# Bias rows and masks made on the chip, and normalisation factors read in longer rows and earlier, in a two-layer kernel

## The chip, the cores and the metric

The kernel runs on one core of one Trainium2 chip. The metric is the device time of one execution in microseconds (us). A core has TensorE (PE, matrix products), VectorE (DVE), ScalarE (ACT), GpSimd (POOL) and SyncE (SP); SP, ACT and POOL also issue transfers (DMA) between DRAM and the on-chip memory SBUF. PSUM holds the results of matrix products. PE's share of full clock that the throttle granted is called the granted clock.

## What is computed

The input `x` is a picture of 512 x 512 positions with 64 channels. Two layers follow one another, each as `x = x + layer(groupnorm(x))`. Only the first layer's part matters here:

```python
xn = _ln(gn(x), norm_w, norm_b)          # over the 64 channels
mask = m[:, :, None] * m[:, None, :]     # m: 0 or 1 for each of 512 rows
left  = (xn @ left_w  + left_b)  * mask * sigmoid(xn @ lgate_w + lgate_b)
right = (xn @ right_w + right_b) * mask * sigmoid(xn @ rgate_w + rgate_b)
out_gate = sigmoid(xn @ ogate_w + ogate_b)
out = einsum('bkjd,bkid->bijd', left, right)
out = _ln(out, onorm_w, onorm_b) @ out_w + out_b
return out * out_gate
```

The second layer takes 12 x 12 low Fourier modes of its input, mixes their channels and transforms them back. Everything is in 32-bit floats.

## The kernel before

About half of the mask is zero, and `left` and `right` vanish wherever a row or column of the mask does. The kernel ranks the rows with a mask of one ahead of the others and gives them *slots*; if there are at most K = 256 of them it takes the path `compact` (line 628), which is the path of every run here. It works in stages that pass their results through DRAM. Within a stage the order of the instructions on each engine is the order of the code (`manual_schedule`): every engine and every queue works off its own list, and waits where a tile that it needs isn't there.

**Indices** (lines 58 to 137, the first 16 us): ranks of the rows by small matrix products, `slot_t` (for each slot the row's number, its mask and Fourier factors) and `src_i` (addresses for gathers).

**Stage 1** (lines 683 to 770): 16 iterations `jc`, each over 32 columns. POOL issues four indirect gathers of 1 MB an iteration (`gather`, L645), two iterations ahead: two into `xg` (the 256 slots), two into `yg` (the other rows). PE transposes all of them (L758) into six PSUM banks, DVE takes statistics of each bank (L759). The slots' columns that have a slot themselves stay in SBUF: `keep` (L740) copies 32 columns of `xg` into `xc`, at addresses read from registers, 22 of them by ACT (SHARE) and 10 by POOL. These dynamic copies write one tile, so ACT's and POOL's batches wait for one another in turn.

Beside that the weights are made. SP loads them (`load_weights`, L148, L167, L168: 28 small transfers). In iterations 5 to 8 ACT scales a weight matrix by the norm's factors (L702) and PE centres it (L707 to L709); in iteration 10 `keep_weights` (L711) copies them out of PSUM, and `b_all`, one column for each of four bias vectors. Two of these (`ogate`, `out`) are also needed as rows, the same in all partitions: SP writes the column to DRAM (`b_d`, L721, 64 writes of 4 bytes) and reads it back to all 128 partitions (`bias_row_...`, L723), twice; then it writes the row of `out` to slot K of `u_d` (L725). In the same way, at the stage's start, the mask of the slots goes from a column of `slot_t` to DRAM (`m_d`, L687, 256 elements of 4 bytes), and back as a row in all partitions (`mask_s`, L688) and as two columns (`mask_own`, L689). SP issues the weights' loads behind these.

**Stage 2** (lines 772 to 916): 64 groups `q` of four slots' columns (each a tile of 128 partitions x 512; a partition is a channel of one of two halves `r`). The loop runs from q = -14 to 63, with `lead` = 13:

- `channels(q+14)` (PE transposes L796, ACT applies the group norm L806),
- `centered(q+13)` (PE L817, ACT squares L821), and DVE sums the squares into `total` (L906),
- after each four groups `factors` puts nine small DVE steps of a reciprocal root on a list `todo`, of which each iteration does three,
- `spread(k)` (QB = 4 groups at once): PE turns the 32 x 128 factors (L834, into the PSUM tile `rc_ps`), ACT copies them (L836), POOL writes them to DRAM (`rs_d`, L838) and reads them back to 64 partitions for each half (`rbc`, L842: 64 x 4 rows of 2 KB for a half, 512 KB), into one of two tiles,
- `normed(q+1)`: DVE multiplies with `rbc` (L849),
- `project`: PE makes `gates` and `sides` (L855), ACT the sigmoid (L880), DVE adds the bias and multiplies (L901), and SP stores `left_d` and `right_d` (L913, 256 KB each) out of one of five tiles `o_c`.

Ahead of the loop the group norm's last steps run (`group_norm_affine`), beside which PE transposes the first six groups (`turn_x`). In the first loop iterations with q >= 0 a list `prepare` is worked off on DVE, one entry each.

**Stage 3** (lines 921 to 982): for each of 64 channels, load both sides (L932), transpose, multiply, mask by `mask_own` and `mask_s` (L967), store to `tri_d`. **Stage 4** normalises that, projects it, gates and adds it to `x` column by column, and takes the Fourier sums on the way; **stage 5** transforms back and writes the output.

Of the kernel before, what the change touches and what calls it, by code (L numbers as in the profile page):

```python
# [17 lines left out]
P = 128  # L18
N = 512
C = 64  # L20
# [11 lines left out]
K = 2 * P  # L32
AHEAD = 15
SHARE = 22
QB = 4
# [11 lines left out]
def conv_preact_kernel(ctx: ExitStack, tc: tile.TileContext, t: dict):  # L47
    nc = tc.nc
    x, out = t["x"], t["out"]

    const = ctx.enter_context(tc.tile_pool(name="const", bufs=1))
    dram = ctx.enter_context(tc.tile_pool(name="dram", bufs=1, space=DRAM))
# [575 lines left out]
    def compact(fc):  # L628
# [53 lines left out]
        with tc.tile_pool(name="wt", bufs=1) as cp:  # L682
            with tc.tile_pool(name="f1", bufs=1) as sp, tc.tile_pool(name="f1x", bufs=2) as xp, tc.tile_pool(
                name="f1y", bufs=4
            ) as yp, tc.tile_pool(name="f1p", bufs=6, space=PSUM) as pt, tc.manual_schedule():
                m_d = dram.tile([K], F32, name="m_d")
                nc.sync.dma_start(m_d.rearrange("(b p) -> p b", p=P), slot_t[:, : K // P, 1])  # L687
                nc.sync.dma_start(mask_s, m_d.unsqueeze(0).to_broadcast([P, K]))  # L688
                nc.sync.dma_start(mask_own, m_d.rearrange("(p b) -> p b", b=2))  # L689
                loaded, _ = load_weights(cp, nc.sync)  # L690
                mkp = ExitStack()
                mk = mkp.enter_context(tc.tile_pool(name="mk", bufs=1, space=PSUM))
# [18 lines left out]
                def keep_weights():  # L711

                    for i, (name, nw, nb, raw, b, k) in enumerate(loaded):
                        weights[name] = raw if i < 2 else fc.tile([P, P], F32, name="w_" + name)
                        nc.scalar.copy(weights[name], made[:, i, :])
                        biases[name] = b_all[:, i : i + 1]
                    nc.scalar.copy(b_all, made_b)
                    mkp.close()
                    b_d = dram.tile([2, C], F32, name="b_d")
                    for i, name in enumerate(("ogate", "out")):  # L720
                        nc.sync.dma_start(b_d[i].rearrange("(c o) -> c o", o=1), biases[name][:C])  # L721
                        rows_of[name] = fc.tile([P, C], F32, name="bias_row_" + name)
                        nc.sync.dma_start(rows_of[name], b_d[i].unsqueeze(0).to_broadcast([P, C]))  # L723
                    for r in range(2):
                        nc.sync.dma_start(u_d[:, K, r, :], rows_of["out"])  # L725

                sets = chunk_sets(fc, 4, 1)
                quarter = NJ // 4
# [15 lines left out]
                for jc in range(NJ):  # L744
                    if jc % quarter == 0:
                        stats = sp.tile([P, 1, 16 * quarter, 6], F32, name="stats1c")
                    if 0 <= jc - 5 < 4:
                        scale_weights(jc - 5)
                    if jc == 10:
                        keep_weights()  # L750
                    for r in range(4):
                        flat = xgs[jc][1][r].rearrange("p j c -> p (j c)")
                        for c in range(4):

                            ps = pt.tile([P, 4, P], F32, name="x_ps")
                            for i in range(4):
                                o = (8 * c + 2 * i) * C
                                nc.tensor.transpose(ps[:, i, :], flat[:, o : o + P], ident)  # L758
# [3 lines left out]
                    if 0 <= jc - 5 < 4:  # L762
                        center_weights(jc - 5)
                    keep(mybir.EngineType.Activation, nc.scalar.copy, jc, 0, SHARE)
                    keep(mybir.EngineType.Pool, nc.gpsimd.tensor_copy, jc, SHARE, JC)
                    del xgs[jc]
                    if jc + 2 < NJ:
                        fetch_tile(jc + 2)
                    if jc % quarter == quarter - 1:
                        join_chunks(sp, sets, jc // quarter, stats)  # L770

            rs_d = dram.tile([K // 4, 2, 4 * P], F32, name="rs_d")
            with tc.tile_pool(name="fn", bufs=2) as np_, tc.tile_pool(name="fw", bufs=2) as wk, tc.tile_pool(
                name="fr", bufs=3
            ) as rp, tc.tile_pool(name="fg", bufs=1) as sp, tc.tile_pool(name="fo", bufs=5) as op, tc.tile_pool(
                name="fpt", bufs=2, space=PSUM
# [33 lines left out]
                def centered(q):  # L810
# [14 lines left out]
                    return sq, totals[k][:, 8 * n : 8 * n + 8]  # L825
# [5 lines left out]
                def spread(k):  # L831

                    ps = spare("rc_ps")[: QB * 8, :P]
                    nc.tensor.transpose(ps, rss.pop(k), ident)  # L834
                    turned = np_.tile([QB * 8, P], F32, name="turned_c")
                    nc.scalar.copy(turned, ps)  # L836
                    groups_d = rs_d[k * QB : (k + 1) * QB]
                    nc.gpsimd.dma_start(groups_d.rearrange("n r (i p) -> (n r i) p", p=P), turned)  # L838
                    rbs[k] = np_.tile([P, QB, N], F32, name="rbc")
                    for r in range(2):  # L840
                        h = slice(r * C, (r + 1) * C)
                        nc.gpsimd.dma_start(  # L842
                            rbs[k][h], groups_d[:, r].unsqueeze(0).to_broadcast([C, QB, N])
                        )

                def normed(q):
                    k, n = divmod(q, QB)
# [11 lines left out]
                def indices(b):  # L859
# [14 lines left out]
                for q in range(-lead - 1, groups):  # L874
                    live = lambda i: 0 <= q + i < groups
                    if live(0):
# [15 lines left out]
                    if 0 <= q < len(prepare):  # L892
# [11 lines left out]
                            )  # L904
                    if live(lead):
                        nc.vector.tensor_reduce(  # L906
                            total.rearrange("p (r i) -> p i r", r=2), sq.rearrange("p (i r) c -> p i r c", r=2), AX.X, ALU.add
                        )
                        if (q + lead) % QB == QB - 1:
                            factors((q + lead) // QB)  # L910
# [687 lines left out]
```

## Time and profile before

| | us |
|---|---|
| median of 3 runs | 1783.5 (1780.29 to 1787.38) |
| profiled execution, its own time | 1782.45 |
| its span, first to last instruction | 1780.7 |
| stage 1 (first gather to POOL's last copy) | 9.8 to 214.1 |
| stage 2 (first transpose to the last group's stores) | 214.1 to 458.7 |
| stage 3, from its first loads | from 461.0 |

| engine | busy us (share of the span) |
|---|---|
| PE | 1557.7 (87%) |
| DVE | 1410.2 (79%) |
| ACT | 947.6 (53%) |
| POOL | 935.4 (53%) |

The profile's page has parts: busy times; the span in 40 equal slices (44.5 us each) with transfer rates and the granted clock; the queues; the chain that ended last; groups of instructions by source line; and transfers. Besides, the trace answers questions: the instructions in order of time (start, duration, engine, line, what is written from what, how many; in brackets the idle time before and what ended it), sums of waits, rates of transfer and busy time in a given stretch. "SPq" and "POOLq" are the queues of transfers of an engine. Line numbers are those of the kernel before, unless said otherwise.

### The profile page before, as it was taken

To read this page: it belongs to the slowest core of one execution; us is meant where nothing else is said; L and a number is where in the kernel's file an instruction comes from. 1 tells how busy PE (TensorE), PEld (TensorE's weight loads), DVE (VectorE), ACT (ScalarE), POOL (GpSimd) and SP (SyncE) were. 2 spreads that over 40 slices of the span, in tenths; PEclk is the share of its full clock that TensorE was granted. 3 is DMA by queue.
4 is the path that set the end of the run, shared out by engine and by line. 5 is a ranking of instruction groups with operands and counts; after the bars stand their busy time and mean duration, and the time that the engine had idled before them with its cause. 6 is when DMAs were issued, how large, how long until landed. Compare 5 with 4: busy or idle time off the path is not lost. (4 is left out here: it accounts for less than half of the span.)

```text
span 1780.7 us, 32739 instructions
## 1 busy us (share of the span) xinstructions
PE 1557.7 (87%) x10918; PEld 1247.9 (70%) x10918; DVE 1410.2 (79%) x2961; ACT 947.6 (53%) x1733; POOL 935.4 (53%) x693
## 2 busy tenths in 40 slices
PE   6775799998899977899999999999999977998772
PEld 5665666654699966788888888888888844665431
DVE  6996878887455558889999999999999984865541
ACT  3664577775233356777777777777777642011000
POOL 3664411111000017789999999999999881111110
PEclk9998999999899999999999999999999976555555
DMA  8999658999799979757876767776777699999998
GB/s 250 388 380 278 244 134 268 279 274 268 233 305 302 304 189 343 259 188 265 300 248 235 273 242 242 253 257 235 258 263 247 216 304 418 426 427 427 426 427 376
DMA packets 193826, 518.68 MB, mean 291 GB/s; under 512 B 38800, under 2 KB 105744, under 8 KB 152688
## 3 DMA queue, kind: packets, MB, share of 16 engines
q1 hardware_dynamic: 157408, 295.92, 47.5%
q0 software_dynamic: 32768, 218.38, 34.7%
q10 hardware_dynamic: 3472, 2.20, 0.5%
q8 instruction: 89, 1.46, 0.3%
q14 instruction: 89, 0.73, 0.1%
HBM read 311.80 MB, written 204.60 MB: 290 GB/s over the span
## 5 line engine op out<-in xcount | busy, mean ns | idle before, releaser
L1109 PE MATMUL w_ps<-gate_x,xt_c 128*128 128x128 f32 x2048 | 279.3, 280 | 30.3 <-DVE z_t L1338 28.6
L1177 POOL TENSOR_TENSOR xc<-xc,z_t 128x1024 f32<-128x1024 f32 x127 | 301.0, 2370 | 8.0
L1109 PEld LDWEIGHTS w_ps<-gate_x,xt_c 128*128 128x128 f32 x2048 | 250.7, 193 | 46.9 <-DVE z_t L1338 45.1
L1109 PE MATMUL c_ps<-center_x,xt_c 128*128 128x128 f32 x2048 | 275.8, 278 | 1.2 <-ACT xt_c L1143 0.6
L1109 PEld LDWEIGHTS c_ps<-center_x,xt_c 128*128 128x128 f32 x2048 | 251.6, 194 | 3.9 <-ACT xt_c L1104 2.8
L1504 PE MATMUL l_ps<-xc,rinv 24*128 24x512 f32 x512 | 208.1, 1136 | 29.5 <-DVE xc L1511 19.7
L1232 DVE BATCH_NORM_STATS2 stats2c<-xc 128x6 f32<-128x128 f32 x1024 | 220.6, 278 | 8.8 <-POOL xc L1177 8.8
L1147 DVE TENSOR_REDUCE scratch<-sq_c 128x16 f32<-128x1024 f32 x160 | 194.6, 1216 | 22.8 <-DMA xc<-tri_d 10.9
L1342 POOL TENSOR_TENSOR z_t<-z_t,bias_row_out 128x1024 f32<-128x1024 f32 x32 | 75.8, 2367 | 249.4 <-DMA xc<-tri_d 227.0
L1285 ACT ACTIVATE z_t<-z_t 128x1024 f32<-128x1024 f32 x128 | 135.5, 1059 | 133.0 <-DVE z_t L1344 132.2
L1504 PEld LDWEIGHTS l_ps<-xc,rinv 24*128 24x128 f32 x512 | 121.1, 306 | 111.5 <-DVE xc L1511 58.1
L759 DVE BATCH_NORM_STATS2 stats1c<-x_ps 128x6 f32<-128x512 f32 x256 | 159.0, 684 | 28.4 <-PE x_ps L758 27.2
L1104 ACT ACTIVATE xt_c<-t_ps,ab_xc 128x512 f32<-128x512 f32 x256 | 175.8, 687 | 9.4 <-PE t_ps L1102 8.4
L1338 DVE TENSOR_TENSOR z_t<-w_ps,rs_n 128x512 f32<-128x512 f32 x256 | 172.0, 672 | 3.0 <-PE w_ps L1109 2.9
L1140 ACT ACTIVATE sq_c<-c_ps 128x512 f32<-128x512 f32 x256 | 150.5, 588 | 27.8 <-PE c_ps L1109 27.3
L1344 DVE TENSOR_TENSOR z_t<-z_t,scratch 128x1024 f32<-128x1024 f32 x128 | 156.3, 1221 | 10.0 <-ACT rs_n L1153 3.7
L1173 POOL TENSOR_TENSOR z_t<-z_t,xc 128x1024 f32<-128x1024 f32 x64 | 151.7, 2370 | 14.5 <-ACT z_t L1285 14.4
L1102 PE MATMUL t_ps<-c_ident,xc 128*128 128x128 f32 x1024 | 157.6, 277 | 0.0
L1102 PEld LDWEIGHTS t_ps<-c_ident,xc 128*128 128x128 f32 x1024 | 117.9, 142 | 52.4 <-issue 52.1
L1511 DVE TENSOR_TENSOR xc<-xc,l_ps 128x512 f32<-128x512 f32 x176 | 109.3, 682 | 57.1 <-DMA xc<-x_h,dst_i 44.8
L1173 POOL TENSOR_TENSOR z_t<-z_t,bias_row_out 128x1024 f32<-128x1024 f32 x63 | 149.8, 2378 | 5.0 <-ACT z_t L1285 4.8
L740 ACT COPY xc<-xg 128x128 f32 x352 | 105.0, 298 | 78.0 <-DMA xg<-in_x,src_i 39.6
(220 smaller groups left out, 2574.5 us busy)
## 6 DMA issues: line engine op xcount, KB each, us to landing
x_h<-xc SPq DMA_DIRECT2D x64, 1024.0 KB
out_x<-xc SPq DMA_DIRECT2D x44, 1024.0 KB
xc<-u_d SPq DMA_DIRECT2D x512, 64.0 KB
out_x<-lx_t SPq DMA_DIRECT2D x20, 1024.0 KB
rbc<-rs_d POOLq DMA_DIRECT2D x32, 512.0 KB, 7.4
left_d<-o_c SPq DMA_DIRECT2D x64, 256.0 KB
right_d<-o_c SPq DMA_DIRECT2D x64, 256.0 KB
left_raw<-left_d SPq DMA_DIRECT2D x64, 256.0 KB
```

The costliest lines, as they stand in the source:

```text
L759: nc.vector.bn_stats(stats[:, 0, 16 * (jc % quarter) + 4 * r + c, :], ps.rearrange("p i k -> p (i k)"))
L1102: nc.tensor.transpose(tps[:, i, :], flat[:, o : o + P], ident)
L1104: nc.scalar.activation(xts[s], tps, AF.Identity, bias=ab1[:, 2:3])
L1109: nc.tensor.matmul(ps[:, 2 * i : 2 * i + 2, :], xts[s][:, i, :], w, start=True, stop=True)
L1140: nc.scalar.activation(sq, cps, AF.Square)
L1147: nc.vector.tensor_reduce(totals[k % 2][:, 8 * (n - 1) : 8 * (n + 1)], sqs.pop(s // 2), AX.X, ALU.add)
L1173: nc.gpsimd.tensor_mul(zs[k, c], zs[k, c], u)
L1177: nc.gpsimd.tensor_add(xr, xr, zs.pop((k, c)))
L1232: nc.vector.bn_stats(st[k // 4][:, g, k % 4, :], x_of(k)[:, :, 2 * g : 2 * g + 2])
L1338: nc.vector.tensor_mul(z[:, 8 * odd : 8 * odd + 8, :], wps, rs)
L1344: nc.vector.tensor_add(z, z, bias_ps["ogate"].unsqueeze(1).to_broadcast([P, 16, C]))
L1504: nc.tensor.matmul(ps.rearrange("p j o -> p (j o)"), rinv[h, b, :], it[h], start=True, stop=True, tile_position=(32 * g, 0),)
```

## The change

It has three parts.

1. *Stage 1.* `m_d` and its two reads, `b_d` and its reads are gone. Instead ACT widens a column to a 128 x 128 tile (`widen`: the two biases, and the two columns of the slots' mask), in iterations 10 to 13; PE multiplies it with the identity (`turn_wide`), which gives the row in all partitions; and in iteration 14 ACT copies the two bias rows and `mask_s` out of PSUM (`keep_wide`). The weights are scaled and centred one iteration earlier (4 to 7, kept in 9). `mask_own` is made in stage 2 by DVE, as a product of `mask_s` with the identity and a sum (`own_of`, entries 2 and 3 of `prepare`). The two writes of the bias row into `u_d` stand behind the stage in the code.
2. *The factors' layout.* `rs_d` holds for each half the factors of four groups in one piece, so that a read is 64 rows of 8 KB. For the first four groups the read is split: the first group's 2 KB rows ahead, then 6 KB rows, four transfers in all. `total`'s columns are ordered to suit. There are three tiles instead of two.
3. *When they are sent.* While q < 0 and from q = 51 on, five instead of three root steps are done in an iteration, and `spread` comes two groups sooner: at q = -8 and -4 (before -6 and -2), and for the last four groups at q = 52 (before 54). In between nothing is moved. Four instead of six groups are transposed beside the group norm.

```diff
@@ stage 1
-                m_d = dram.tile([K], F32, name="m_d")
-                nc.sync.dma_start(m_d.rearrange("(b p) -> p b", p=P), slot_t[:, : K // P, 1])
-                nc.sync.dma_start(mask_s, m_d.unsqueeze(0).to_broadcast([P, K]))
-                nc.sync.dma_start(mask_own, m_d.rearrange("(p b) -> p b", b=2))
...
+                def widen(i):
+                    column = biases[("ogate", "out")[i]] if i < 2 else slot_t[:, i - 2, 1:2]
+                    scales[i] = cp.tile([P, P], F32, name=f"wide{i}", tag="scaled")
+                    nc.scalar.copy(scales[i], column.to_broadcast([P, P]))
+                def turn_wide(i):
+                    nc.tensor.matmul(made[:, i, :], scales.pop(i), ident, start=True, stop=True)
+                def keep_wide():
+                    for i, name in enumerate(("ogate", "out")):
+                        rows_of[name] = fc.tile([P, C], F32, name="bias_row_" + name)
+                        nc.scalar.copy(rows_of[name], made[:, i, :C])
+                    nc.scalar.copy(mask_s, made[:, 2:4, :].rearrange("p b k -> p (b k)"))
                     mkp.close()
-                    b_d = dram.tile([2, C], F32, name="b_d")
-                    for i, name in enumerate(("ogate", "out")):
-                        nc.sync.dma_start(b_d[i].rearrange("(c o) -> c o", o=1), biases[name][:C])
-                        rows_of[name] = fc.tile([P, C], F32, name="bias_row_" + name)
-                        nc.sync.dma_start(rows_of[name], b_d[i].unsqueeze(0).to_broadcast([P, C]))
-                    for r in range(2):
-                        nc.sync.dma_start(u_d[:, K, r, :], rows_of["out"])
...
-                    if 0 <= jc - 5 < 4:
-                        scale_weights(jc - 5)
-                    if jc == 10:
+                    if 0 <= jc - 4 < 4:
+                        scale_weights(jc - 4)
+                    if jc == 9:
                         keep_weights()
+                    if 0 <= jc - 10 < 4:
+                        widen(jc - 10)
+                    if jc == 14:
+                        keep_wide()
...
+                    if 0 <= jc - 10 < 4:
+                        turn_wide(jc - 10)
@@ stage 2
-            rs_d = dram.tile([K // 4, 2, 4 * P], F32, name="rs_d")
-            with tc.tile_pool(name="fn", bufs=2) as np_, ...
+            rs_d = dram.tile([K // 4 // QB, 2, QB, 4 * P], F32, name="rs_d")
+            with tc.tile_pool(name="fn", bufs=3) as np_, ...
...
-                    for r in range(2):
-                        h = slice(r * C, (r + 1) * C)
-                        nc.gpsimd.dma_start(
-                            rbs[k][h], groups_d[:, r].unsqueeze(0).to_broadcast([C, QB, N])
-                        )
+                    flat = rbs[k].rearrange("p n k -> p (n k)")
+                    for o in (slice(0, N), slice(N, QB * N)) if k == 0 else (slice(0, QB * N),):
+                        for r in range(2):
+                            h = slice(r * C, (r + 1) * C)
+                            nc.gpsimd.dma_start(
+                                flat[h, o], rs_d[k, r].rearrange("n k -> (n k)")[o].unsqueeze(0).to_broadcast([C, o.stop - o.start])
+                            )
...
+                def own_of(b):
+                    own = sp.tile([P, P], F32, name=f"own{b}", tag="wide")
+                    nc.vector.tensor_mul(own, mask_s.rearrange("p (q b) -> p b q", b=2)[:, b], ident)
+                    nc.vector.tensor_reduce(mask_own[:, b : b + 1], own, AX.X, ALU.add)
-                prepare = [lambda: indices(0), lambda: indices(2)]
+                prepare = [lambda: indices(0), lambda: indices(2), lambda: own_of(0), lambda: own_of(1)]
...
-                    fc, sets, 2 * stats.shape[2], "xc", with_variance=lambda ab: [turn_x(q) for q in range(6)],
+                    fc, sets, 2 * stats.shape[2], "xc", with_variance=lambda ab: [turn_x(q) for q in range(4)],
...
+                for r in range(2):
+                    nc.sync.dma_start(u_d[:, K, r, :], rows_of["out"])
...
-                    for step in todo[:3]:
+                    some = 5 if q < 0 or q + lead >= groups else 3
+                    for step in todo[:some]:
                         step()
-                    del todo[:3]
+                    del todo[:some]
...
-                    if live(lead - QB) and (q + lead - QB) % QB == QB - 1:
-                        spread((q + lead - QB) // QB)
+                    early_by = 2 if q < 0 or q + lead >= groups else 0
+                    if live(lead - QB + early_by) and (q + lead - QB + early_by) % QB == QB - 1:
+                        k = (q + lead - QB + early_by) // QB
+                        if k in rss:
+                            spread(k)
```

More of the change, by code (lines that the diff above doesn't have):

```diff
@@ L761, in compact @@
                             )
-                    if 0 <= jc - 5 < 4:
-                        center_weights(jc - 5)
+                    if 0 <= jc - 4 < 4:
+                        center_weights(jc - 4)
+                    if 0 <= jc - 10 < 4:
+                        turn_wide(jc - 10)
                     keep(mybir.EngineType.Activation, nc.scalar.copy, jc, 0, SHARE)
@@ L770, in compact @@
                         join_chunks(sp, sets, jc // quarter, stats)
-            rs_d = dram.tile([K // 4, 2, 4 * P], F32, name="rs_d")
-            with tc.tile_pool(name="fn", bufs=2) as np_, tc.tile_pool(name="fw", bufs=2) as wk, tc.tile_pool(
+            rs_d = dram.tile([K // 4 // QB, 2, QB, 4 * P], F32, name="rs_d")
+            with tc.tile_pool(name="fn", bufs=3) as np_, tc.tile_pool(name="fw", bufs=2) as wk, tc.tile_pool(
                 name="fr", bufs=3
@@ L824, in centered @@
                         totals[k] = rp.tile([P, QB * 8], F32, name="total")
-                    return sq, totals[k][:, 8 * n : 8 * n + 8]
+                    return sq, totals[k].rearrange("p (r n i) -> p n i r", r=2, n=QB)[:, n]
                 def factors(k):
@@ L836, in spread @@
                     nc.scalar.copy(turned, ps)
-                    groups_d = rs_d[k * QB : (k + 1) * QB]
-                    nc.gpsimd.dma_start(groups_d.rearrange("n r (i p) -> (n r i) p", p=P), turned)
+                    nc.gpsimd.dma_start(rs_d[k].rearrange("r n (i p) -> (r n i) p", p=P), turned)
                     rbs[k] = np_.tile([P, QB, N], F32, name="rbc")
-                    for r in range(2):
-                        h = slice(r * C, (r + 1) * C)
-                        nc.gpsimd.dma_start(
-                            rbs[k][h], groups_d[:, r].unsqueeze(0).to_broadcast([C, QB, N])
-                        )
+                    flat = rbs[k].rearrange("p n k -> p (n k)")
[5 more added lines that the diff above has]
+                            )
                 def normed(q):
@@ L906, in compact @@
                         nc.vector.tensor_reduce(
-                            total.rearrange("p (r i) -> p i r", r=2), sq.rearrange("p (i r) c -> p i r c", r=2), AX.X, ALU.add
+                            total, sq.rearrange("p (i r) c -> p i r c", r=2), AX.X, ALU.add
                         )
```

## The prediction, made before the changed kernel ran

> **What bounds the kernel now.** I read the page's slices first, then the list of waits for the first 210 us, then the timeline of each place where the waits are long, then the transfer rate and the granted clock there.
>
> The page's row of transfer rates (one number for each 44.5 us) falls in its fourth to sixth slice, in stages that move megabytes:
>
> ```profile
> GB/s 250 388 380 278 244 134 268 279 274 268 233 305 302 304 189 343 259 188 265 300 248 235 273 242 242 253 257 235 258 263 247 216 304 418 426 427 427 426 427 376
> ```
>
> The waits up to 210 us (total, times, longest) say who suffers: the keeping copies and the transposes of stage 1 wait for gathered tiles, and 10 us at once is far over the usual.
>
> ```profile
> ACT xc L740 <- DMA xg<-in_x,src_i: 39.6, 7, 10.3
> PE x_ps L758 <- DMA yg<-in_x,src_i: 24.7, 22, 6.3
> ```
>
> The timeline from 130 to 172 us places it:
>
> ```profile
> 132.46 0.47 SPq L721 DMA_DIRECT2D b_d<-b_all  x1
> ...
> 143.30 5.65 PE L758 MATMUL x_ps<-c_ident,yg 128*128 128x128 f32 x32 [6.12 <-DMA yg<-in_x,src_i]
> 144.11 0.33 SPq L723 DMA_DIRECT2D bias_row_ogate<-b_d  x1
> 144.49 0.74 SPq L721 DMA_DIRECT2D b_d<-b_all  x1
> ...
> 152.62 7.27 ACT L740 COPY xc<-xg 128x128 f32 x22 [10.10 <-DMA xg<-in_x,src_i]
> ...
> 160.78 0.33 SPq L723 DMA_DIRECT2D bias_row_out<-b_d  x1
> 160.91 3.63 PE L758 MATMUL x_ps<-c_ident,yg 128*128 128x128 f32 x16 [6.32 <-DMA yg<-in_x,src_i]
> ```
>
> L723 reads what L721 wrote, so its issue marks the landing of 64 writes of 4 bytes: 11.6 and 16.3 us after their issue. Both times the gathers revive in the same moment. The rate from 131 to 165 us (40 slices of 0.85 us) shows two holes of 7 to 9 slices, each ending at such a landing:
>
> ```profile
> GB/s 395 434 405 405 424 434 434 405 202 19 10 58 96 77 67 48 48 19 241 414 453 400 378 431 410 415 424 77 58 39 116 125 145 145 48 29 39 222 405 414
> ```
>
> A third hole (22 to 175 GB/s) lies at 16.5 to 22.5 us, and the wait of SP's queue for `m_d` (L687, 256 elements of 4 bytes) ends at 22.0. I read all three as one thing: 4-byte writes to DRAM block the gathers for some 6 us.
>
> Stage 2 has two places where DVE waits for the factors (L849), and after each the granted clock (column PEclk) is half:
>
> ```profile
> 239.67 0.69 DVE L849 TENSOR_TENSOR xnc<-xc,rbc 128x512 f32<-128x512 f32 x1 [2.68 <-DMA rbc<-rs_d]
> ...
> 444.60 0.69 DVE L849 TENSOR_TENSOR xnc<-xc,rbc 128x512 f32<-128x512 f32 x1 [5.65 <-DMA rbc<-rs_d]
> ```
>
> ```profile
> 237.00:240.40 3.40, 0.00 (x0) 0.00 (x0) 0.73 (x2) 1.88 (x2) 0.37 (x1) 0.87 0.40 75
> 240.40:246.00 5.60, 5.58 (x18) 3.53 (x20) 2.55 (x11) 2.53 (x4) 0.87 (x2) 0.50 0.84 186
> ```
>
> ```profile
> 445.00:450.00 5.00, 4.56 (x12) 2.23 (x12) 2.93 (x6) 1.26 (x2) 0.00 (x0) 0.50 0.45 120
> ```
>
> Between them a group takes 3.40 us (gates at 322.09, 325.49, 328.88), PE busy without a gap: nothing in the change lightens that.
>
> **The change, part by part.** The stages follow one another through DRAM, so what a stage ends sooner reaches the end. All sums are made against the profiled execution (1782.45 us, span 1780.7, 1.75 around it); the median of the three runs is 1783.5, so I take them as one.
>
> *(a) The two `b_d` writes go.* Iterations of stage 1 start (ACT L740) at 124.48, 135.29, 152.62, 170.21, 181.54, 192.36 us. The undisturbed step is 10.87: 7.23 us of ACT's 22 copies, then 3.48 us of POOL's 10, which wait for one another, plus 0.15. The three long steps are over by 6.46, 6.72 and 0.46: **13.6 us**. What is late next is this ACT-POOL chain itself; DVE has 16 x 0.62 us = 9.9 in each. Added here: four widening copies and three keeping copies on ACT (L715 shows 0.26 to 0.29 us for 128x128, so about 2 us in all) and four matmuls of 0.39 us (L707's row). They run while ACT waits for POOL's 3.48 us and PE for DVE (0.5 us before each batch); uncovered they would cost 3.6. `wide` has one buffer, so a widening copy waits for the preceding matmul; behind it on ACT stand the next 22 copies. The same pair on L702/L707 ran with 1 us to spare (97.7 against 98.7, next copies 102.6). I take 0.
>
> *(b) The `m_d` round trip goes.* The first copies start at 25.38 because the second gathered tile lands at 24.0. Up to 16.5 us the gathers had moved about 1.6 MB; the two tiles that ACT needs are 2 MB, so without the hole they are there at about 17.5; with the table load (1.28) ACT starts at 18.8. SP's 28 small loads then start at about 7 instead of 23 us, on top of the first gathers. Their price at this place is not in the trace; between 23 and 58 us no hole stood beside them. Bounds 0 (they eat it all) and 6.9; I take **6.0**, by the nearest row, the undisturbed rates after 24 us.
>
> *(c) Start of stage 2.* Two of six early transposes (0.8 us each at half clock) move behind the first centred groups: 0.8 us sooner. Nine root steps in two iterations (5+4) instead of three: DVE has 1.0 + 0.69 us in an iteration of 1.33, so the root is ready only 0.6 us sooner, though PE's order allows 2.7. `spread(0)` now turns through `rc_ps` between two centred groups that use it: PE waits for ACT's copy once, about 0.9 lost. Then 128 KB for each half carries group 0 instead of 512 KB. In the trace the pair was issued at 232.18 and DVE freed at 239.67; 1 MB moved there in some 4.7 us, steady at about 215 GB/s, so a quarter takes 1.2 us. Written at 228.3, read from 230.5, the first pair is there at about 234, before PE's last centred group at 236. Gates of group 0 then follow without a gap, the clock stays up, and group 1's gates come at ACT's table load and two sigmoids, about 239.9, instead of 246.69: **6.8**. Bounds 4.0 (the wait goes, the half clock stays) and 7.5. POOL issues 4 reads of 0.62 us where it had 2; behind them waits `rs_d(1)`, needed at 246, some 2 us to spare.
>
> *(d) Steady part.* Three tiles instead of two and longer rows change no PE work: 0. One wait of 1.1 us for the factors may go: **+1.1**. `own_of` puts two products (as L867, 0.28) and two sums (as L248, 0.32) on DVE in groups 2 and 3, where it has 0.25 us to spare: **-0.6** (0 to -1.3).
>
> *(e) End of stage 2.* Group 60 needed its factors at 438.7 and got them at 444.60; with the half clock after it the last gates stand at 454.17 instead of about 445.7, so 8.5 us are there. The last `spread` moves from q=54 to 52: its root is ready at 424.95, ACT's copy behind a sigmoid at 426.6, POOL's write at 427.0 instead of 429.51. If the way from there takes 15.1 us as before, the data land at 442.1: 2.5 us sooner, a stall of 3.4. What row length does is not shown for this read. The nearest row is the loads of `tri_d` at 640 to 656 us, 64 partitions with 4-KB rows: 240 GB/s beside 215 for the factors' 2-KB rows, so at best a tenth of 9 us is won. I take a stall of 2.4 and the clock saved in 6 of 10 cases: 3.4 + 1.6 = **5.0**, bounds 2.5 and 8.5.
>
> [...]
>
> Sum: 13.6 + 6.0 + 6.8 + 1.1 - 0.6 + 5.0 = 31.9; 1782.45 - 31.9 = **1750.5**.
>
> **Rivals.**
> *A, a hole stays in stage 1.* SP runs ahead: the two `u_d` writes (256-byte rows) wait only for ACT's bias row in iteration 14, so they are still issued among the last gathers, and stage 1 keeps 28 small loads. If they make one hole of 6.4 us: 1757. Against it: before, the same writes were issued at 169.08, and the rate from 165 to 182 us is 416 GB/s without a hole. [...]
> *B, the factors come no sooner at the end*, because the write waits behind the preceding 1-MB read in POOL's ring: (e) is 0, 1755.5.
> *C, the holes were not of the writes' making* and the gathers stall anyway: (a) and (b) go, 1782.45 - 12.3 = 1770.
> *D, slower.* The steady loop's transfers become the bound: with rows of 8 KB between the stores of `left_d` and `right_d` (4 KB), the five result tiles `o_c` come free late and DVE L901 waits. A group moves 768 KB, 226 GB/s at 3.40 us. The loss passes the 31.9 gained at 4.03 us for each of some 50 groups and makes the kernel slower by over 0.5% at 4.2, about 1792. Against it: no wait of L901 for a transfer in the trace, and the bytes stay the same.
>
> **How the numbers follow.** Chances: forecast 0.66, A 0.11, B 0.10, C 0.08, D 0.05. The bounds together give 1782.45 - 37.6 = 1745 and 1782.45 - 18.8 = 1763.5; with the spread of the runs (1780.3 to 1787.4) the range is 1740 to 1766, holding A and B. A measurement of this kernel can tell some 0.5% (8.9 us) from no change: faster 0.91, same 0.04, slower 0.05.
>
> **What would show it.** (a) no step between ACT's L740 batches over 11.5 us; (b) the first batch at 18 to 20 us; (c) stage 1 over near 194, group 1's gates near 220 (246.69 before), and no half clock at group 0; (d) 3.40 us a group; (e) wait of L849 near the end 0 to 3.4 us. Wrong would be: holes in the rate where no 4-byte write is, a first batch near 25 us, or L901 waiting for stores.

## The result and the profile after

The changed kernel takes 1763.4 us (median of 4 runs, 1759.8 to 1765.6), before 1783.7 (1780.3 to 1787.4): the ratio is 0.988, with a 95% interval of 0.986 to 0.991. A second series gave 1765.5 us and 0.989 (0.988 to 0.991). The forecast was 1750.5, the range 1740 to 1766. The time is inside the range and faster as forecast, but some 12 us of the forecast gain are missing. The profiled execution took 1764.03 us (span 1762.2), 18.4 less than the profiled 1782.45 of before, where the sum had promised 31.9. The 13.5 us between the two are what has to be accounted for. Line numbers from here on are those of the kernel whose profile is shown.

I read it in the order of the prediction. The row of transfer rates on the page first (one number for each 44.1 us):

```profile
GB/s 282 392 388 370 145 186 289 283 262 258 305 305 303 246 256 343 197 237 289 245 248 260 245 240 248 259 250 241 247 263 245 218 311 423 424 427 426 426 428 363
```

The fourth slice, 278 before, is now 370: stage 1 moves at one rate almost to its end. The waits of the first 210 us (total, times, longest) agree. ACT's longest wait for a gather was 10.3 us and is 4.0, PE's was 6.3 and is 2.3:

```profile
PE x_ps L768 <- DMA xg<-in_x,src_i: 17.8, 18, 2.3
...
ACT xc L746 <- DMA xg<-in_x,src_i: 15.1, 4, 4.0
PE x_ps L768 <- DMA yg<-in_x,src_i: 10.6, 17, 1.1
```

The rate from 131 to 165 us, where two holes stood, has none:

```profile
GB/s 414 405 299 173 357 395 337 337 386 318 386 405 414 443 424 434 270 299 395 347 308 405 357 366 405 405 414 424 424 299 337 405 318 337 376 299 386 424 453 395
```

Stage 1 (to POOL's last copy) ends at 197.86 us instead of 214.06. But the gates of group 1 start 31.9 us after that, hardly less than the 32.6 of before. The timeline of the start of stage 2 shows why (start, duration, engine and line; in brackets the idle time before and what ended it):

```profile
209.89 0.19 DVE L218 SCALAR_TENSOR_TENSOR rq_w<-rq_w,rq_y 128x32 f32<-128x32 f32 x1
210.12 0.19 DVE L219 SCALAR_TENSOR_TENSOR rq_out<-rq_w,rq_y 128x32 f32<-128x32 f32 x1
210.45 0.27 PE L846 MATMUL rc_ps<-c_ident,rq_out 128*32 128x128 f32 x1 [2.22 <-DVE rq_out L219]
210.76 0.25 ACT L848 COPY turned_c<-rc_ps 32x128 f32<-32x128 f32 x1 [1.66 <-PE rc_ps L846]
211.07 1.16 PE L829 MATMUL rc_ps<-c_center,xc 128*128 128x128 f32 x8 [0.34 <-ACT turned_c L848]
...
212.70 1.91 PE L829 MATMUL cc_ps<-c_center,xc 128*128 128x128 f32 x8
...
220.42 0.28 PE L846 MATMUL rc_ps<-c_ident,rq_out 128*32 128x128 f32 x1 [2.13 <-DVE rq_out L219]
...
229.76 1.02 PE L868 MATMUL gates_c<-xnc,raw_gates 64*128 64x512 f32 x4
```

The last line is the gates of group 1; before it was this one:

```profile
246.69 1.02 PE L855 MATMUL gates_c<-xnc,raw_gates 64*128 64x512 f32 x4
```

`spread`, two groups sooner, is a new wait: its transpose (L846) stands in PE's list before products that are ready, and PE stands still until DVE's nine steps (L209 to L219) are through. Everything on ACT and DVE in this stretch feeds on PE, so they stand too. Behind the first wait eight products (L829) take 1.91 instead of 1.06 us. The table of stretches (PE, PEld, DVE, ACT, POOL busy, then PEclk, DMA share, GB/s) gives the clock:

```profile
208.00:212.00 4.00, 1.44 (x12) 1.03 (x10) 2.07 (x10) 1.36 (x3) 0.39 (x1) 1.00 0.00 0
212.00:216.00 4.00, 4.00 (x24) 4.00 (x23) 1.38 (x2) 2.47 (x4) 2.25 (x5) 0.57 0.20 55
```

The half clock that this part of the change was to remove is back, here behind the first of the two waits. At the end of stage 2 the same wait stands a third time, but there the long wait for the factors (5.65 us) is gone; group 60's product starts as soon as DVE is free:

```profile
407.26 0.40 PE L846 MATMUL rc_ps<-c_ident,rq_out 128*32 128x128 f32 x1 [2.54 <-DVE rq_out L219]
...
423.68 0.68 DVE L862 TENSOR_TENSOR xnc<-xc,rbc 128x512 f32<-128x512 f32 x1
```

By stretches, between marks that both profiles have, the two profiled executions compare so:

| stretch | before, us | after, us | gained | predicted |
|---|---|---|---|---|
| to ACT's first copies (b) | 25.38 | 21.80 | 3.6 | 6.0 |
| from there to the end of stage 1 (a) | 188.68 | 176.06 | 12.6 | 13.6 |
| from there to the gates of group 1 (c) | 32.63 | 31.90 | 0.7 | 6.8 |
| groups 1 to 51, steady (d) | 171.72 | 170.83 | 0.9 | 0.5 |
| from there to the last store's issue (e) | 39.73 | 35.16 | 4.6 | 5.0 |
| from there to the end of the span | 1322.5 | 1326.5 | -4.0 | 0 |

So 6 us are missing at (c), 2.4 at (b), 1.0 at (a), and 4 behind stage 2, where the change does nothing.

### The profile page after: what moved, and what is told of

It reads as the page before. It is cut to its first block, busy times and chain, and to the rows that moved or that the text cites. A ratio compares the mean times of both kernels' runs of the same rounds, so it can differ in the third digit from the quotient of the medians.

```text
span 1762.2 us, 32746 instructions
## 1 busy us (share of the span) xinstructions
PE 1555.0 (88%) x10926; PEld 1245.0 (71%) x10926; DVE 1409.0 (80%) x2965; ACT 949.0 (54%) x1740; POOL 932.7 (53%) x695
## 5 line engine op out<-in xcount | busy, mean ns | idle before, releaser
L1528 PE MATMUL l_ps<-xc,rinv 24*128 24x512 f32 x512 | 208.8, 1136 | 29.0 <-DVE xc L1535 18.8
L1171 DVE TENSOR_REDUCE scratch<-sq_c 128x16 f32<-128x1024 f32 x160 | 194.8, 1218 | 23.1 <-ACT sq_c L1166 18.4
L1368 DVE TENSOR_TENSOR z_t<-z_t,scratch 128x1024 f32<-128x1024 f32 x128 | 156.3, 1221 | 10.3 <-ACT rs_n L1177 3.7
```

Source lines behind the costliest of these rows:

```text
L1171: nc.vector.tensor_reduce(totals[k % 2][:, 8 * (n - 1) : 8 * (n + 1)], sqs.pop(s // 2), AX.X, ALU.add)
L1368: nc.vector.tensor_add(z, z, bias_ps["ogate"].unsqueeze(1).to_broadcast([P, 16, C]))
L1528: nc.tensor.matmul(ps.rearrange("p j o -> p (j o)"), rinv[h, b, :], it[h], start=True, stop=True, tile_position=(32 * g, 0),)
```

## Experiments

The theory N: TensorE's order makes the early `spread` a wait, and with the half clock it costs the 6 us of (c). Its rival R1: the factors' transfers bound the start, so an early place can only help. For the 4 us behind stage 2 there are R2 and K (the later stages give back what is won, or the change costs them something) and V (they scatter). Times below are medians; a ratio is to the kernel before, run beside it on the same chip, with its 95% interval.

**Only the start move undone.**

```diff
-                    early_by = 2 if q < 0 or q + lead >= groups else 0
+                    early_by = 2 if q + lead >= groups else 0
```

> The changed kernel with one part undone: at the start spread stands at its old place (early_by 0 for q < 0), at the end two groups sooner as changed. Theory N: the gates of group 1 come near 25 us after the end of stage 1 instead of 33.7, no half clock between 212 and 216 us, the wait of 2.5 us at q = 52 stays; time 8 to 9 us below the changed kernel, 1754 to 1756. Rival R1 (the early factors were worth their wait): 1763 or more.

Measured: 1758.4 us, ratio 0.986 (0.984 to 0.988), beside 1765.5 for the changed kernel on the same chip: 7 us less, where 8 to 9 had been expected. (The expectation's 33.7 should read 31.9, by the rows above.) The gates of group 1 come 25.4 us after the end of stage 1, and the same transposes wait for nothing:

```profile
210.92 0.27 PE L846 MATMUL rc_ps<-c_ident,rq_out 128*32 128x128 f32 x1
...
216.35 0.27 PE L846 MATMUL rc_ps<-c_ident,rq_out 128*32 128x128 f32 x1
...
223.45 1.02 PE L868 MATMUL gates_c<-xnc,raw_gates 64*128 64x512 f32 x4
```

The same two stretches in this kernel, with PE busy throughout and the clock full:

```profile
208.00:212.00 4.00, 4.00 (x38) 3.99 (x37) 3.51 (x13) 3.85 (x7) 0.00 (x0) 1.00 0.02 4
212.00:216.00 4.00, 4.00 (x38) 4.00 (x37) 2.97 (x13) 3.83 (x7) 1.91 (x4) 1.00 0.04 10
```

This is the plainest proof: one line undone gives 6.5 us in this stretch (31.9 to 25.4). The two waits are 4.35 us of it; the turn-round of `rc_ps` (0.34) and the half clock come on top, and a run below tells the clock's share.

**The old place everywhere.** `early_by = 0`, all else as changed.

> The changed kernel with spread at its old place everywhere (early_by 0); five root steps, three tiles, long rows and the split of group 0 stay. Theory N: no wait of TensorE at the factors' transpose; at the start the factors' first 128 KB land near 218.5, when they are just needed, so the gates of group 1 come near 223.5 (229.8 in the changed kernel); at the end the wait at group 60 is back, some 4 to 5.5 us, with half clock. Time within 3 us of the changed kernel: 1760 to 1766. Rival R1 (the transfers bound both places): start 2.7 us later and end 5 us later than in the changed kernel: 1770 to 1772.

Measured: 1764.6 us, 0.989 (0.987 to 0.991), the time that N expected, but not by N's sum. Gates of group 1 at 221.1, 24.9 us after the end of stage 1; the three waits of L846 are gone. The end of stage 2 loses: the wait for the factors is back, with half clock behind it.

```profile
416.54 0.69 DVE L862 TENSOR_TENSOR xnc<-xc,rbc 128x512 f32<-128x512 f32 x1 [3.09 <-DMA rbc<-rs_d]
417.37 2.06 PE L868 MATMUL gates_c<-xnc,raw_gates 64*128 64x512 f32 x4 [2.75 <-DVE xnc L862]
```

So the early place pays at the end and costs at the start. From the gates of group 51 to the last store's issue this kernel takes 37.4 us, the one with only the start undone 34.5: at the end the early place is worth 2.9 us. The two don't cancel: from the end of stage 1 to the last store's issue the changed kernel takes 237.9 us and this one 233.5. In the profiled execution these 4.4 us were lost again behind stage 2, which took 1328.5 us from the first loads of stage 3 to the end, against 1323.5. That the time came out as N expected is partly luck.

**Behind PE's own products.** `spread` one group sooner and behind `centered` at the start, two groups sooner and behind `sides` at the end.

```diff
+                    early_by = 1 if q < 0 else 2 if q + lead >= groups else 0
+                    if due and early_by == 0:
+                        spread(k)
...
                         sides = project(q, "sides")
+                    if due and early_by > 0:
+                        spread(k)
```

> The changed kernel with spread put behind TensorE's own products: at the start one group sooner than the old place and behind centered, at the end two groups sooner and behind sides. Theory N: the three waits of the transpose shrink to under 0.7 us each, no half clock at 212 to 215 us, the gates of group 1 come 6 to 7 us sooner (near 223 instead of 229.8); at the end up to 2.5 us go, but the factors of group 60 land at about 422.5 and a wait of 0 to 2.5 us comes back there. Time 6 to 9 us below the changed kernel: 1754 to 1757. Rival R1 (the factors' transfers bound the start): a wait of L862 of about 6 us for rbc appears at group 0 and the time stays at 1761 to 1764.

Measured: 1756.1 us, 0.985 (0.983 to 0.987). Gates of group 1 at 223.07, the start 25.1 us; R1's wait of some 6 us for the factors doesn't show (the longest at the start is 1.12 us). At the end L846 waits 0.26 us instead of 2.54, and the 1.60 us that it leaves over come back as a wait for the factors, as expected:

```profile
401.04 0.28 PE L846 MATMUL rc_ps<-c_ident,rq_out 128*32 128x128 f32 x1 [0.26 <-DVE rq_out L219]
...
416.77 0.69 DVE L862 TENSOR_TENSOR xnc<-xc,rbc 128x512 f32<-128x512 f32 x1 [1.60 <-DMA rbc<-rs_d]
```

**One part alone.** Stage 1 changed and stage 2 as before; then the reverse.

> Stage 1 of the changed kernel (no b_d, no m_d), stage 2 of the kernel before, with own_of and the two u_d writes added. Theory N (the missing part of the gain is a new wait of TensorE in the changed stage 2): stage 1 ends near 198 us as in the changed kernel (214.1 before), stage 2 runs as before (gates of group 1 32.6 us after the end of stage 1, a wait of some 5.6 us at group 60), time about 16 us below before: 1766 to 1770. Rival R2 (stage 1 itself gave less than its 16 us to the end, because later stages give it back): the stages from 800 us on run some 4 to 6 us longer here too, and the time is 1772 or more.

Measured: 1776.3 us, 0.994 (0.992 to 0.996). This is not what N expected, but R2's number. Stage 1 ends at 199.3, 14.7 us sooner, and the last store of stage 2 is issued 13.8 us sooner (the wait at group 60 is 7.10 instead of 5.65 us). What is missing beyond that was lost behind stage 2: 1328.3 us from the first loads of stage 3 to the end, against 1319.7.

> Stage 1 of the kernel before (with b_d and m_d), stage 2 of the changed kernel without own_of. Theory N: TensorE stands 2.2, 2.1 and 2.5 us at its three early transposes of the factors; the start of stage 2 gains under 1 us and the end 5 to 6, so the time is 5 to 8 us below before: 1775 to 1779. By the prediction's own terms (c) and (e) it would be 12 us below: 1771 to 1773. Rival R2: the later stages give it back and the time is within 3 us of before.

Measured: 1778.7 us, 0.996 (0.995 to 0.998), 5.4 us less, as N expected. The transpose (L834 here) waits 2.22, 2.13 and 2.54 us as well, to the hundredth as in the changed kernel: the waits come with the order, not with stage 1. But behind the first two the clock stays full (below, the stretch of the first wait, the one behind it, and the one behind the second):

```profile
227.80 0.27 PE L834 MATMUL rc_ps<-c_ident,rq_out 128*32 128x128 f32 x1 [2.22 <-DVE rq_out L219]
...
236.13 0.28 PE L834 MATMUL rc_ps<-c_ident,rq_out 128*32 128x128 f32 x1 [2.13 <-DVE rq_out L219]
...
245.48 1.02 PE L856 MATMUL gates_c<-xnc,raw_gates 64*128 64x512 f32 x4
```

```profile
224.00:228.00 4.00, 1.78 (x16) 1.44 (x14) 2.90 (x11) 2.39 (x4) 0.00 (x0) 1.00 0.00 0
228.00:232.00 4.00, 3.65 (x33) 3.58 (x33) 1.12 (x2) 2.58 (x5) 1.63 (x4) 1.00 0.04 8
236.00:240.00 4.00, 3.87 (x35) 3.87 (x36) 1.45 (x3) 2.78 (x5) 1.53 (x3) 1.00 0.20 44
```

This prices the half clock. From the first waiting transpose to the gates of group 1 this kernel takes 17.7 us (227.80 to 245.48), the changed kernel, with half clock for 3.41 us, 19.3 (210.45 to 229.76). So of the 6.5 us at the start about 1.6 are the half clock, and the waits alone cost the other 4.9.

Up to the last store's issue the two parts alone win 13.8 and 6.3 us, 20.1 together, of the 22.4 of the whole change. In the medians they win 7.9 and 5.4 of 20.3; what differs does not lie in stages 1 and 2.

**Both kernels a second time**, for the stages behind stage 2.

> The changed kernel once more, unchanged, for the scatter of the stages behind stage 2. Theory V (the later stages, from the first loads of stage 3 to the end, scatter by some us from execution to execution): they took 1319.7 us in the profile of before and 1323.5 in that of the changed kernel; a second profile of it gives another value between 1320 and 1329, and stages 1 and 2 repeat within 1 us (gates of group 1 at 229 to 231). Rival K (the change itself costs them 4 us): 1323 to 1324 again, and before 1319 to 1320 again.

> The kernel before once more, for the same: theory V: its later stages take another value between 1320 and 1329; rival K: 1319 to 1320 again.

Measured: in its second profile the changed kernel has the same three waits, its start takes 32.9 us (31.9 in the first), and the half clock lies behind the second wait (the stretch behind the first wait, then the one behind the second):

```profile
211.96 0.27 PE L846 MATMUL rc_ps<-c_ident,rq_out 128*32 128x128 f32 x1 [2.22 <-DVE rq_out L219]
...
220.28 0.28 PE L846 MATMUL rc_ps<-c_ident,rq_out 128*32 128x128 f32 x1 [2.13 <-DVE rq_out L219]
```

```profile
214.00:218.00 4.00, 4.00 (x38) 3.92 (x36) 2.25 (x5) 3.81 (x7) 2.11 (x4) 1.00 0.36 76
222.00:226.00 4.00, 4.00 (x25) 4.00 (x25) 1.38 (x2) 2.45 (x5) 1.02 (x2) 0.64 0.50 123
```

From the first loads of stage 3 to the end of the span: the changed kernel 1323.5 and again 1323.5, before 1319.7 and then 1322.6. The other ten profiles of this study have 1321.8 to 1328.5, in no order that follows their edits: 1328.5 with the old place, 1324.5 with half of it. So 2.9 of the 4 us are within the scatter of one kernel. That the change costs these stages 1 to 3 us is neither shown nor excluded (mean of before 1321.1, of all others 1324.3, two profiles against twelve). In the medians the two kernels differ by 20.3 and 20.5 us, 2 less than the 22.4 won up to the last store in the first pair of profiles; the second pair won 21.0 there.

**Stage 1: the small loads.** SP is held until the second gathered tile has landed, by a write of 128 rows of 256 bytes out of it.

```diff
-                loaded, _ = load_weights(cp, nc.sync)
...
+                hold_d = dram.tile([P, C], F32, name="hold_d")
+                nc.sync.dma_start(hold_d, xgs[0][0][:, 1, 0, :])
+                loaded, _ = load_weights(cp, nc.sync)
```

> The changed kernel with SP held until the second gathered tile has landed (SP first writes 128 rows of 256 bytes of it to a scratch tensor), so that none of the 28 small loads stands beside the first two gathers. Theory S (the small loads, above all the 4-byte ones between 8 and 16 us, take the missing 2.4 us of the first batch): the gap in the gathers at 14.9 to 16.5 us is gone, the first copies of ACT start at 19.4 to 20.4 instead of 21.8 us, stage 1 ends 1.4 to 2.4 us sooner, time 1761 to 1762.5. Rival G (the gathers alone need that long): first copies at 21.6 to 22.0 and the time within the scatter of the changed kernel.

Measured: 1764.2 us, 0.989 (0.987 to 0.991); first copies at 20.58 instead of 21.80, stage 1's end at 195.4 instead of 197.9. The rates from 6 to 27 us, in the changed kernel and then here (0.53 us a number):

```profile
GB/s 0 0 0 0 1 0 1 0 0 1 141 109 265 421 406 390 234 31 0 16 299 462 384 430 405 405 445 396 395 413 386 431 351 426 382 397 426 398 429 385
```

```profile
GB/s 0 0 0 0 0 0 0 0 0 0 187 94 281 359 468 406 343 218 343 374 390 312 390 406 406 406 406 437 421 406 406 426 407 434 419 417 424 422 406 422
```

The gap of 31, 0, 16 at about 15 us is gone, so S is right on the gap, and half right on the first batch: of the 2.4 us that (b) missed, some 1.2 are the loads' and the rest are the two gathers' own (without the hold, eight profiles have the first copies at 21.6 to 22.6). For the end of the stage it isn't shown: seven profiles with the changed stage 1 as it is end it at 196.2 to 199.3. In the time it doesn't show either: the later stages took 1325.5 us.

**Stage 1: one 4-byte write put back**, into nothing that is read.

```diff
                         keep_weights()
+                        hole_d = dram.tile([C], F32, name="hole_d")
+                        nc.sync.dma_start(hole_d.rearrange("(c o) -> c o", o=1), b_all[:C, 2:3])
```

> The changed kernel with one write of 64 elements of 4 bytes to a scratch tensor added in iteration 9 of stage 1, which nothing waits for. Theory H (4-byte writes hold up the gathers): one hole of 5 to 8 us in the transfer rate behind the write, one step of ACT's batches about 6 us longer, stage 1 ends 5 to 6.7 us later, time 1768 to 1771. Rival C (the holes were of another making): no hole, time as the changed kernel.

Measured: 1772.4 us, 0.994 (0.992 to 0.996), and stage 1's end 7.2 us later. The write, the wait behind it and the rate from 118 to 145 us (0.68 us a number):

```profile
119.08 0.47 SPq L758 DMA_DIRECT2D hole_d<-b_all  x1
```

```profile
139.64 7.24 ACT L746 COPY xc<-xg 128x128 f32 x22 [10.31 <-DMA xg<-in_x,src_i]
```

```profile
GB/s 291 328 413 388 425 413 425 437 401 389 85 12 0 0 85 24 73 73 61 49 49 49 12 182 364 449 413 437 413 425 449 413 437 413 425 449 413 437 413 425
```

64 writes of 4 bytes make one hole and one step of 17.73 instead of 10.81 us: 6.9 us, beside 6.46 and 6.72 in the kernel before. C is out. `u_d`'s rows of 256 bytes (at 172.67 us in the changed kernel) and the 256-byte rows of `hold_d` made no hole: the rate is 345 to 416 GB/s in every 2 us from 172 to 184, and 406 to 437 from 19.3 to 27 us in the run with the loads held.

**Row length of the factors.** 2-KB rows as before, all else as changed.

> The changed kernel with the factors in rows of 2 KB as before (rs_d by groups), all else as changed, the early places too. Theory (row length wins nothing): the last 1-MB read of factors takes about as long as in the changed kernel (7 us from its first to its last packet), no wait of L862 at group 60 over 1 us, time within 2 us of the changed kernel, 1761 to 1766. Rival L (row length sets the rate): the read takes 8.5 us as before, a wait of 1 to 2.5 us appears at group 60, time 1765 to 1768.

Measured: 1771.0 us, 0.993 (0.991 to 0.995). The last read takes 6.4 us from its first to its last packet, 7.2 with the long rows (by the trace's records of packets), and no wait stands at group 60; so far the theory. But a wait that the prediction's (d) had named, and that the changed kernel lost, is back and larger, at group 40 (1.10 us in the kernel before; with long rows no profile has more than 0.51 there):

```profile
363.81 0.69 DVE L862 TENSOR_TENSOR xnc<-xc,rbc 128x512 f32<-128x512 f32 x1 [1.98 <-DMA rbc<-rs_d]
```

So the long rows win (d)'s 1.1 us in the steady part, and nothing at the end; why the short ones are late just there isn't told apart. This wait explains 2 of the 5 to 8 us by which the median is above the changed kernel's. The profiled execution (1765.3) was faster than the other three, and the rest stays open.

**Put together.** The old place at the start, behind `sides` at the end, the last factors split like the first, the loads held, and a copy of one column on ACT at 6.6 us, which brings its table load (1.28 us) forward; then the same with the last 16-KB write of factors issued by ACT.

```diff
+                warm = sp.tile([P, 1], F32, name="warm")
+                nc.scalar.copy(warm, ident[:, :1])
...
-                    for o in (slice(0, N), slice(N, QB * N)) if k == 0 else (slice(0, QB * N),):
+                    for o in (slice(0, N), slice(N, QB * N)) if k in (0, K // 4 // QB - 1) else (slice(0, QB * N),):
```

> Put together: spread at its old place at the start, two groups sooner and behind sides at the end, the last block of factors split as the first one is (128 KB for each half first), small loads held as in e5, and one small copy on ACT at the start, so that its table is loaded before the first tile is there. Theory N and S: against e3 the start of stage 2 is 2 us better (gates of group 1 near 25 us after the end of stage 1), the wait of 1.6 us at group 60 goes, stage 1 ends some 3 us sooner: 1748 to 1752. If S is wrong, 1.3 us at most for the table: 1751 to 1755. Rival: what is won ahead is given back in the later stages, and the time stays at e3's 1756.

```diff
-                    nc.gpsimd.dma_start(rs_d[k].rearrange("r n (i p) -> (r n i) p", p=P), turned)
+                    (nc.scalar if k == K // 4 // QB - 1 else nc.gpsimd).dma_start(rs_d[k].rearrange("r n (i p) -> (r n i) p", p=P), turned)
```

> e8 with the last write of factors (16 KB) issued by ACT instead of POOL, so that it goes by a queue of its own. Rival B of the prediction held that this write waits behind the 1-MB read ahead of it in POOL's ring: then the last reads are issued 2 to 2.6 us after the write instead of 5.6, and the wait of 1.5 us at group 60 goes. If the write is slow for another reason, the 5.6 us and the wait stay. In the time 1.5 us at most, 1753 to 1755 by e8's median, less than the scatter: the trace decides.

Measured: 1755.1 us, 0.984 (0.982 to 0.986), and 1755.9 us, 0.984 (0.983 to 0.986). Both are below the changed kernel (their intervals and that of its second series, 0.988 to 0.991, don't meet; that of its first series, from 0.986 on, touches them); against the 1756.1 of `spread` behind PE's products they can't be told apart, and 1748 to 1752 was too much to expect. In the first, stage 1 ends at 193.5 (in the second, with the same stage 1, at 196.5) and the last stores come 4.7 us sooner than with `spread` behind PE's products alone; a wait of 1.47 us for the factors is left at group 61, since group 60's piece was there in time. ACT's own queue did not help: the last reads are issued 5.6 us after the write with either queue, and DVE stands 1.22 us at the same place.

```profile
399.82 0.36 ACTq L853 DMA_DIRECT2D rs_d<-turned_c  x1
...
405.41 2.05 POOL L859 DMA_DIRECT2D rbc<-rs_d  x4 [8.73 <-DVE o_c L932]
```

At the start of stage 2, where nothing else moves, the same step takes 2.0 us. In the changed kernel, by the trace's records of packets, the write issued at 408.23 moved at 411.0 to 412.6, as those of the 1-MB read ahead ran out (411.3). In the kernel before, that read had ended (429.47) when the write was issued (429.51), and the step still took 4.84 us, beside stores. So the step is long with either queue, POOL's ring is not the cause, and that the read is the cause is not shown.

## Why the prediction was right and wrong

- **(a)** Right: 12.6 of 13.6 us. Holes are the 4-byte writes' making (one put back costs 6.9), and the added work on ACT and PE cost nothing that can be seen; what is missing is of the size of the four steps in which ACT still waits for a gather, 0.3 to 0.9 us over 10.87 each (two of them, 11.54 and 11.75, pass the 11.5 that was set as the sign), and less than the scatter of this stretch (174.2 to 177.4 us in seven profiles with the same stage 1). The prediction misread two details of the row of rates: the holes are 9 and 10 slices long, not 7 to 9, and the rate came back at 146.3 and 162.4 us, some 2 us behind the two landings and not in the same moment.
- **(b)** Mechanism right, size wrong: 3.6 instead of 6.0, inside its bounds. The small loads, which now stand on top of the first gathers, took some 1.2; the estimate of when two tiles are there (17.5 us) was 1.8 too early even without them (19.3). Its own terms give 6.6 as the upper bound (25.38 less 18.8), not 6.9.
- **(c)** Wrong: 0.7, under its lower bound of 4.0. The failed step is "the root is ready only 0.6 us sooner, though PE's order allows 2.7". It was worked out when the factors could come; that PE, which works in order, would stand in that difference was not. I priced a wait at this place for `rc_ps` (0.9) and none for the root. The rest of (c) (the first read in two pieces, five root steps, four early transposes; no run tells them apart) does what the move was meant to do: without the move it gains 7.2 us (32.6 to 25.4). That this is near the 6.8 forecast is partly chance, since the forecast counted the early factors, and 1 us is scatter (31.9 and 32.9 in the two profiles of the changed kernel). The move itself costs 6.5.
- **(d)** Right in sign and size: 0.9 for 0.5. The 1.1 us wait went, by the row length; `own_of` cost nothing that the steady groups show.
- **(e)** Right in sum, 4.6 for 5.0, wrong in its parts: no stall of 2.4 was left at group 60, but PE's wait of 2.54 came at q = 52 instead, by the same slip as in (c). The 8-KB rows, for which the stall of 2.4 counted up to 0.9 us, won nothing here: the last read takes 7.2 us with them and 6.4 with rows of 2 KB.
- **Behind stage 2** I counted nothing; the profiled pair lost 4.0, of which 2.9 lie within what one kernel shows.
- **The range.** That the time lies inside it is partly luck. 1763.4 is nearly what the lower bounds of all parts together give (1763.5), but (c) fell below its bound and 4 us were lost where nothing was counted, while the other parts came nearer their forecasts.
- **Rivals.** A came true in none of its forms (`u_d` made no hole, the loads cost 1.2 and not 6.4). B is half borne out: the reads come 5.6 us after the write, but on ACT's queue as well, and (e) was gained all the same. C is refuted. D's wait (L925 for stores) doesn't appear: 3.40 us a group (768 KB in that time are 231 GB/s, not 226). The case that happened, a wait on DVE that takes the place of the wait for a transfer, was none of them.

Between 195 and 459 us of the two first profiles the trace's records of the granted clock show half clock for 3.41 us or twice that: 3.41 three times and 6.83 once in the changed kernel, 6.83 three times before. What brings the clock down these runs don't show. In the changed kernel it fell behind a wait of 2.22 us, with PE busy for 1.44 of 4 us around it, and stayed up behind one of 2.13; in the second profile of the same kernel it was the other way about, and in the kernel with stage 2 alone changed it fell behind neither. So the length of the wait alone did not decide it.

## What to carry to other kernels

Before an instruction is moved ahead on an engine that works in order, compare the time at which its input is ready with the time at which the engine arrives there: the difference is a wait of everything that stands behind it. An early place pays where it removes a longer wait than it makes, as at the end of stage 2 (2.54 us in place of 5.65), and ready products put ahead of the moved step cover its wait (0.26). Small writes of 4 bytes between bulk transfers are worth removing even when nothing waits for them, since here 64 of them held up the gathers by 6.5 to 6.9 us.

## Not expected of the hardware

64 writes of 4 bytes, for which nothing waits, stop a stream of some 400 GB/s for about 8.5 us, and the stop begins 5.5 to 9.5 us after their issue. The same two waits (2.22 and 2.13 us) brought the clock down once in each profile of one kernel, but not at the same one, and not at all in another kernel. From a 16-KB write to the reads behind it 5.6 us passed near the end of stage 2, whichever of two engines' queues it went by, and 2.0 us at its start, where nothing else moved.
